# Two-layer graph network on one Trainium2 core: Layer 0 counts its first 208 edge tiles, edge attributes are turned before they are masked, and a node block's tables are made in one burst

## The chip, the cores and the metric

The kernel runs on one core of one Trainium2 chip. The metric is the device time of one execution in microseconds (us), lower is better. Engines are called as in the profile: PE (TensorE matmul), PEld (its weight loads), DVE (VectorE), ACT (ScalarE), POOL (GpSimd), SP (the engine that here only issues DMAs).

## The reference

There are 3,125 nodes with 128 features and 100,000 edges, sorted by destination. The destinations are drawn as 3125·u² with u uniform, so low node numbers have very many edges (node 0 alone has over 1,700) and the destinations advance slowly at first. Cut to what matters:

```
# Layer 0: mean of the source rows, one linear layer, ELU, residual, layer norm
summed = segment_sum(x[src], dst);  deg = segment_sum(1, dst)
x = layernorm(x + elu((summed / max(deg, 1)) @ W + b))
# Layer 1: relational attention, R = 4 edge types, H = 4 heads of C = 128 (HC = 512)
xl = x @ W_l[r] + b_l[r];  xr = x @ W_r[r] + b_r[r]            # tables, one row per node and type
e  = edge_attr @ W_e[type, :16] + rel_emb[type] @ W_e[type, 16:]
z  = leaky_relu(xl[src, type] + xr[dst, type] + e, 0.2)
score = sum_c z[h, c] * att[type, h, c]
alpha = softmax of score over the edges with one (dst, type)
agg[dst, type] += alpha * xl[src, type]
# mean over heads, a softmax gate over types, layer norm, FFN, two layer norms
```

## The kernel before

Edges are cut into 784 tiles of 128, four of them a **quad** (196 quads). The function `windows` has four stages.

**Prologue.** Index arrays are loaded, turned so that an edge lies on a partition (`src_e`, `loc_e`, `typ_e`), and a flag is worked out that says whether the index data satisfy what the fast path assumes. If not, a general path runs after it.

**Layer 0**, a loop over steps `s`, one quad a step. POOL gathers the 128 source rows of each tile by an indirect DMA into a ring `xg` of 24 tiles (`gather`). A one-hot of the destinations (`onehot4`, tile `oh`) multiplies the gathered rows (`sums0`, PSUM tile `sg`), ACT copies the sums (`sgs`), a second one-hot (`spread0`, `ohq`) spreads them to 64 nodes (`out0`, PSUM tile `fo`), and DVE adds that to the running sums of all nodes (`add0`, `acc0`). `sums0` of a quad frees its four ring places, and only then are the next four gathers issued.

Beside that the same loop prepares Layer 1:
- Edge attributes: `load_chunk` loads 112 tiles' attributes at a time (`earow`, seven chunks; the last has 109 full rows), `turn_chunk` transposes them and splits each into a high and a low part, 32 values an edge (`ees`). For each quad `masked` copies the 32 values to the four types' places and zeroes those of the other types (DVE, `em`, 128 x 512), `turned` transposes the four tiles (four PE transposes into `mp`, an ACT copy to `emt`), and `keep` writes 256 KB to DRAM (`eam_d`).
- Node blocks: as soon as the sums of 128 nodes are complete (`behind(b)` says after which quad), `block` runs its parts in following steps: `take`, `mean` (linear layer on PE), an exponential on ACT, `stats`, a square root on ACT, `scaled`, `turn` (transpose to `ht`). Then `lin` makes 16 columns and `table(r)`, one type a step, makes the two tables of a type: two matmuls 128x128x512 into `xp`, a DVE addition of the bias `cl` to the left one, a DVE addition of `cb` to the right one (`xf`), an ACT rounding of it (`xh`), and a step later in `half(r)` DVE's remainder. The tables go to DRAM (`xl_d`, `xr_d`).

The order on each of PE, DVE, ACT, POOL and SP is written out by hand: the class `Ordered` chains all instructions of an engine in the order in which the program issues them (all have line 647 in the profile). Jobs are put at a step by `at_step`.

**Attention**, again one quad a step, in a software pipeline. `load_rows` loads for the next quad the masked attributes `ea` (four buffers), the segment row `sg` (three buffers), `rm` and the windows of the right table `win` (14 buffers), all on SP's queue; `load` gathers the left table's rows on POOL. For each head `z_of` sums on PE two attribute matmuls (`weh`, `wel` by `ea`), the window matmuls by the one-hot `oht` and four transposes, into one of three PSUM tiles `z`; ACT applies `relu`; PE makes the scores (`row`). DVE does the softmax by scans (`local1` .. `joined4`), PE and DVE the weighted sums.

**Tail**: the final norms and the feed-forward layer over 25 node blocks.

Of the kernel before, what the change touches and what calls it, by code (L numbers as in the profile page):

```python
# [20 lines left out]
P = 128  # L21
# [640 lines left out]

def windows_of(u):
    k = 4 if u < UQ else 2 if u < UP else 1
    return [(i, k) for i in range(0, 4, k)]
# [15 lines left out]
def windows(ctx: ExitStack, tc: tile.TileContext, a, out, flag):  # L681
# [7 lines left out]
    eam_d = dram.tile([NQ, P, 512], F32, name="eam_d")  # L689
# [5 lines left out]
    xli_e = S["xli_e"] = cst.tile([P, TT], I32, name="xli_e")  # L695
# [10 lines left out]
    tng = cst.tile([P, TT, R], BF16, name="tng")  # L706
# [35 lines left out]
    with tc.tile_pool(name="l0c", bufs=1) as l0c:  # L742
        acc0 = l0c.tile([P, 2, NPW], F32, name="acc0")
        src_e = l0c.tile([P, TT], I32, name="src_e")

        XG = 24
        xg = l0c.tile([P, XG, F + 1], F32, name="xg")
        nc.vector.memset(xg[:, :, F:], 1.0)
        pool = Ordered(tc, nc.gpsimd)
# [5 lines left out]
        with tc.tile_pool(name="pr", bufs=1) as pr, tc.tile_pool(name="prp", bufs=2, space=PSUM) as prp:  # L755
# [26 lines left out]

            srci = rows("srci", "src", 0, nc.scalar)
# [7 lines left out]
            bad = pr.tile([P, 8], F32, name="bad")  # L791
# [3 lines left out]
            nc.vector.memset(acc0, 0.0)  # L795

            src = floats("src", srci)
            to_e(src_e, src)
            for t in range(XG):
                gather(t)  # L800
# [25 lines left out]
            rF, rL, rB = (rfl[:, i] for i in range(3))  # L826
            wt = prp.tile([TR, TC], F32, name="fp_")
# [9 lines left out]
            nc.vector.tensor_copy(d0_i, rB[0:1])  # L837
            typ = floats("typ", typi)
            to_e(typ_e, typ)
            tm = l0c.tile([P, TT, R], BF16, name="tmr")  # L840
# [5 lines left out]
            nc.vector.scalar_tensor_tensor(seg, loc, float(R), typ, op0=OP.mult, op1=OP.add)  # L846
# [23 lines left out]
            rF4, rL4 = (x[0:1].rearrange("p (u i) -> p u i", i=4) for x in (rF, rL))  # L870
            for j, (w, x, y) in enumerate((
# [4 lines left out]
                count(1 + j, n)  # L876

# [7 lines left out]
            bp = prp.tile([1, 8], F32, name="bp", bufs=1)  # L885
# [18 lines left out]
        with tc.tile_pool(name="m0c", bufs=1) as m0c, tc.tile_pool(name="l0", bufs=2) as l0, \  # L904
# [4 lines left out]
            one = l0e.tile([1, 1], F32, name="one")  # L909
            nc.vector.memset(one, 1.0)  # L910
# [12 lines left out]
            fb = l0e.tile([P, TT], F32, name="fb")  # L923
# [4 lines left out]
            cl = m0c.tile([P, R, XW], F32, name="cl")  # L928
            cb = m0c.tile([P, R, HC], F32, name="cb")
# [11 lines left out]
            def load_table_weights():  # L941
# [4 lines left out]
                sp.dma_start(cl[:, :, :HC], bass.AP(tensor=a["L1_gnn_b_l"].tensor, offset=a["L1_gnn_b_l"].offset,  # L946
                                                    ap=[[0, P], [HC, R], [1, HC]]))
# [30 lines left out]
            def rows_of_sources():  # L978

                ve.tensor_scalar_min(xli_e, typ_e, float(R - 1))  # L980
                ve.scalar_tensor_tensor(xli_e, src_e, R, xli_e, op0=OP.mult, op1=OP.add)
                ve.tensor_scalar(tng, tm, 1.0, BIG, op0=OP.subtract, op1=OP.mult)

            def linear_weights(r, w):
                def f():
# [3 lines left out]
                    tmp = m0.tile([P, HC], F32, name="tmp", bufs=1)  # L989
                    ve.tensor_mul(tmp, w[:, r, :HC], at_)  # L990
                    ve.tensor_reduce(w[:, r, HC:XW], tmp.rearrange("p (h c) -> p h c", h=H), AX.X, OP.add)
                    ve.tensor_scalar(w[:, r, HC:XW], w[:, r, HC:XW], SLOPE, None, op0=OP.mult)
                return f

            def constant(r):
                def f():
# [3 lines left out]
                    cp = bank().rearrange("p a b -> p (a b)")  # L1000
                    pe.matmul(cp, cr[:, r:r + 1].to_broadcast([DR + 1, P]), cw, start=True, stop=True)
                    act.activation(cb[:, r], cp, AF.Copy)
# [3 lines left out]
            for i, f in enumerate([edge_weights, rows_of_sources] +  # L1006
                                  [linear_weights(r, w) for r in range(R) for w in (wl, cl)] +
                                  [constant(r) for r in range(R)]):
                at_step(4 + i, "ve", f)
# [186 lines left out]
            for s in range(last + 1):  # L1196
# [3 lines left out]
                if s < NQ:  # L1200
                    turned(s)
# [484 lines left out]
```

## Time and profile before

| | |
|---|---|
| median of 3 runs | 3265.17 us (3262.53 to 3267.92) |
| the profiled execution | 3014.4 us, span 3012.6 us |
| mean granted TensorE clock in the profiled execution | 0.851 |
| prologue, to the first `sg` matmul | 64.3 us |
| Layer 0, first to last `sg` matmul | 64.3 to 1154.7 us |
| first `z` matmul of attention | 1236.5 us |
| last addition of attention | 2892.1 us |

The profiled execution is 250.8 us shorter than the median of the timed runs. Busy times and durations below are of the profiled execution. In a window's answer a row gives each engine's busy time and, in brackets, its number of instructions; a float32 matmul is shown as two instructions.

### The profile page before, as it was taken

To read this page: it belongs to the slowest core of one execution; us is meant where nothing else is said; L and a number is where in the kernel's file an instruction comes from. 1 tells how busy PE (TensorE), PEld (TensorE's weight loads), DVE (VectorE), ACT (ScalarE), POOL (GpSimd) and SP (SyncE) were. 2 spreads that over 40 slices of the span, in tenths; PEclk is the share of its full clock that TensorE was granted. 3 is DMA by queue.
4 is the path that set the end of the run, shared out by engine and by line. 5 is a ranking of instruction groups with operands and counts; after the bars stand their busy time and mean duration, and the time that the engine had idled before them with its cause. 6 is when DMAs were issued, how large, how long until landed. Compare 5 with 4: busy or idle time off the path is not lost.

```text
span 3012.6 us, 69650 instructions
## 1 busy us (share of the span) xinstructions
PE 2521.1 (84%) x25681; PEld 1858.9 (62%) x25681; DVE 1794.3 (60%) x6092; ACT 867.3 (29%) x1872; POOL 1552.6 (52%) x1578
## 2 busy tenths in 40 slices
PE   2867777767567777699999999999999999999952
PEld 1444444434244343477777777888888888788832
DVE  6523445455455565367666667667666666566667
ACT  1212223233233232233333333333333333233211
POOL 5777777777756650444444444444444444444200
PEclk9555667677767687899999999999999999999956
DMA  5433545465445554777777777888888899999710
GB/s 154 141 111 98 162 140 184 162 202 186 154 172 191 174 185 169 271 225 221 221 227 221 222 224 231 256 257 255 255 258 252 255 260 259 245 253 258 189 34 23
DMA packets 278166, 599.24 MB, mean 199 GB/s; under 512 B 47142, under 2 KB 98647, under 8 KB 273820
## 3 DMA queue, kind: packets, MB, share of 16 engines
q1 hardware_dynamic: 186568, 334.42, 34.2%
q0 software_dynamic: 87808, 258.61, 30.5%
q8 instruction: 206, 3.38, 0.5%
q10 hardware_dynamic: 3440, 1.66, 0.3%
q14 instruction: 144, 1.17, 0.1%
HBM read 460.02 MB, written 134.48 MB: 197 GB/s over the span
## 4 chain that ended last, share of the span: by engine, by line
PE 50%; DMA 6%; DVE 3%; issue 0%; SPq 0%; ACT 0%; DVEq 0%; ACTq 0%
PE z L647 30%; PE row L647 9%; PE ag L647 6%; DMA win<-xr_d 4%; PE fo L647 2%; PE sm_p L647 2%; DMA ea<-eam_d 1%; DMA out_dram<-o 0%; DMA fh_all<-fh_d 0%; DMA rm<-rm_d 0%; PE hm L1640 0%; DVE fst L1599 0%; PE xp L647 0%; DMA xr_d<-xh 0%; SPq L647 0%
## 5 line engine op out<-in xcount | busy, mean ns | idle before, releaser
L647 POOL DMA_INDIRECT xl<-xl_d,xli_e x784 | 754.0, 962 | 958.3 <-DVE r L647 326.1
L647 POOL DMA_INDIRECT xg<-in_x_dram,src_e x784 | 797.4, 1017 | 323.0 <-issue 132.0
L647 ACT ACTIVATE relu<-z 128x512 f32<-128x512 f32 x784 | 468.4, 597 | 1104.5 <-PE z L647 1102.7
L647 PE MATMUL z<-f_ident,xl 128*128 128x128 f32 x3136 | 475.6, 274 | 0.0
L647 PEld LDWEIGHTS z<-f_ident,xl 128*128 128x128 f32 x3136 | 368.5, 141 | 44.5 <-issue 0.6
L647 PE MATMUL z<-ea,weh 128*128 128x512 f32 x784 | 383.9, 490 | 12.6 <-DMA sg<-seg_d 12.6
L647 PE MATMUL z<-oht,win 96*128 96x128 f32 (+2 forms) x1600 | 346.9, 298 | 16.5 <-DMA win<-xr_d 16.2
L647 PEld LDWEIGHTS z<-oht,win 128*128 128x128 f32 (+1 forms) x1600 | 276.8, 190 | 77.0 <-DMA win<-xr_d 10.3
L647 PE MATMUL z<-ea,wel 128*128 128x512 f32 x784 | 311.3, 397 | 0.0
L647 PE MATMUL fo<-ohq,sgs 128*128 128x64 f32 x784 | 168.3, 357 | 164.2 <-ACT sgs L647 68.5
L647 PE MATMUL sg<-xg,oh 128*32 128x129 f32 x1568 | 200.6, 361 | 122.8 <-DMA xg<-in_x_dram,src_e 120.7
L647 PEld LDWEIGHTS fo<-ohq,sgs 128*128 128x128 f32 x784 | 153.7, 274 | 193.0 <-ACT sgs L647 130.7
L647 PE MATMUL row<-relu,attw 128*32 128x128 f32 x6272 | 248.5, 276 | 0.0
L647 PEld LDWEIGHTS sg<-xg,oh 128*32 128x32 f32 x1568 | 64.5, 126 | 281.6 <-DMA xg<-in_x_dram,src_e 184.3
L647 DVE TENSOR_TENSOR oh<-loc_e,iw 128x128 f32<-128x128 bf16 (+1 forms) x294 | 99.1, 337 | 217.1 <-PE sg L647 216.7
L647 PE MATMUL ag<-xl,wo 128*32 128x128 f32 x6272 | 218.8, 280 | 3.4 <-DVE wo L647 3.4
L647 PEld LDWEIGHTS z<-ea,weh 128*128 128x128 f32 x784 | 148.1, 189 | 89.6 <-issue 89.5
L647 PE MATMUL mp<-f_ident,em 128*128 128x128 f32 x784 | 178.8, 369 | 11.0 <-issue 5.1
L647 ACT ACTIVATE xh<-xf 128x512 fp32r<-128x512 f32 x100 | 63.0, 630 | 431.5 <-DVE xf L647 257.1
L647 PEld LDWEIGHTS row<-relu,attw 128*32 128x32 f32 x6272 | 164.0, 110 | 32.7 <-issue 32.7
L647 PEld LDWEIGHTS ag<-xl,wo 128*32 128x32 f32 x6272 | 164.4, 112 | 7.2 <-DVE wo L647 3.7
L647 DVE TENSOR_TENSOR acc<-acc,fo 128x128 f32 (+1 forms) x392 | 99.5, 254 | 115.0 <-issue 44.1
(270 smaller groups left out, 3602.4 us busy)
## 6 DMA issues: line engine op xcount, KB each, us to landing
win<-xr_d SPq DMA_DIRECT2D x224, 256.0 KB
xr_d<-xh SPq DMA_DIRECT2D x100, 512.0 KB
eam_d<-emt SPq DMA_DIRECT2D x196, 256.0 KB
ea<-eam_d SPq DMA_DIRECT2D x196, 256.0 KB
win<-xr_d SPq DMA_DIRECT2D x176, 192.0 KB
xl_d<-xlr SPq DMA_DIRECT2D x25, 1032.0 KB
sg<-seg_d SPq DMA_DIRECT2D x196, 128.0 KB
rm<-rm_d SPq DMA_DIRECT2D x392, 32.1 KB
```

What stands on the lines that cost most here:

```text
L647: ins = f(*args, **kw)
```

## The change

- **Counting.** For the first 52 quads (`UD`, 208 tiles; all destinations below `ND` = 240) no rows are gathered. `count` makes for each tile a one-hot of the source's low 7 bits (`ol`, 128 x 128) and one of the pair source block and destination (`oc`, 128 x 200, from quad 24 on 128 x 300), and one bf16 matmul a tile counts into PSUM `dn`; `count_add` adds a quad's counts to a matrix `A` (128 x 25 x 252) at a column read into a register. When all are counted, `counted_sums` multiplies the 25 blocks of `x` with `A` and adds the result to `acc0`. The flag gets three more conditions. The Layer 0 loop has 144 steps for the other quads; the 52 counts are put on steps 3 to 41, two, one and one to a step; the multiplications follow from step 43 on, and blocks 0 and 1 come after them.
- **Attributes turned unmasked.** One transpose turns a quad's four tiles of 32 values; four quads share one ACT copy and are written as four DMAs of 64 KB (`eat_d`). In attention a load repeats the 32 rows for the four types (`er`, two buffers), ACT makes the distance of the segment row from the row's type (`far`, one buffer), and DVE's `masked` multiplies by a comparison of it (`ea`, now two buffers).
- **Tables in one burst.** All eight table matmuls of a block come in one step (`tables`), each preceded by a matmul that adds the bias from a two-part float32r row (`two`, `cbl`). ACT copies the tables out of PSUM (`xh`, `xlr`), the DVE additions go, the four `half` come in the next step between DVE's other work, and `xl_d` is written in four DMAs.
- **Order.** ACT's copy of the last quad's sums (`out_copy`) comes first in the next step.

```
+UD, ND, SHI = 52, 240, NB2
+def counted(u):
+    return 8 if u < 24 else 12
...
-            for t in range(XG):
+            for t in range(TD, TD + XG):
                 gather(t)
...
-            def masked(u):
...
-            def turned(u):
-                mp, m = bank(), X.pop(("em", u))
-                for q in range(4):
-                    pe.transpose(mp[:, q], m[:, q].rearrange("p r x -> p (r x)"), ident)
-                em = X["emt", u] = l0.tile([P, 4, P], F32R, name="emt", bufs=4)
+            def turned(us):
+                mp = bank()
+                for j, u in enumerate(us):
+                    c, i0 = u // QC, u * 4 % TR
+                    pe.transpose(mp[:, j], ees[c][:, i0:i0 + 4].rearrange("p t s d -> p (t s d)"), ident)
+                em = l0.tile([P, 4, P], F32R, name="emt", bufs=3)
                 act.activation(em, mp, AF.Copy)
...
+            def count(u):
+                w = counted(u)
+                cn = l0p.tile([P, SHI, w], F32, name="dn")
+                for i in range(4):
+                    t = 4 * u + i
+                    ol = l0.tile([P, P], BF16, name="ol", bufs=4)
+                    ve.tensor_scalar(ol, il, lo_f[:, t:t + 1], None, op0=OP.is_equal)
+                    oc = l0.tile([P, SHI * w], BF16, name="oc", bufs=4)
+                    ve.tensor_scalar(oc, ic[:, :SHI * w], c_f[:, t:t + 1], None, op0=OP.is_equal)
+                    pe.matmul(cn.rearrange("p a b -> p (a b)"), ol, oc, start=(i == 0), stop=(i == 3))
+            def count_add(u):
+                n = nc.values_load(dc_i[0:1, u:u + 1], engines=[ENG.DVE], min_val=0, max_val=ND - 1, ...)
+                v = A[:, :, ds(n, counted(u))]
+                ve.tensor_tensor(v, v, X.pop(("cn", u)), op=OP.add)
+            def counted_sums(k):
+                pe.matmul(X["dn"][:, 0], X.pop(("xc", k)), A[:, k, :ND], start=(k == 0), stop=False, ...)
...
+            C0 = 3
+            for u in range(UD):
+                at_step(C0 + u * 3 // 4, "count", u)
...
-                def lin():
-                def table(r):
-                    ve.tensor_add(d["xlr"][:, r, :HC], xp, cl[:, r, :HC])
-                    ve.tensor_add(d["xf", r], xq, cb[:, r])
-                    act.activation(d["xh", r][:, 0], d["xf", r], AF.Copy)
+                def tables():
+                    xa = m0p.tile([P, R, H], F32, name="mw")
+                    pe.matmul(xa, two[:, 0], cbl[:, :, HC:], start=True, stop=False)
+                    pe.matmul(xa, d["ht"], wl[:, :, HC:], start=False, stop=True)
                     for r in range(R):
+                        xp, xq = (m0p.tile([P, HC], F32, name="xp", bufs=3) for _ in range(2))
+                        for o, w, i, c in ((xq, wr[:, r], 1, cbl[:, r, :HC]), (xp, wl[:, r, :HC], 0, cbl[:, r, :HC])):
+                            pe.matmul(o, two[:, i], c, start=True, stop=False)
+                            pe.matmul(o, d["ht"], w, start=False, stop=True)
+                        act.activation(xh[:, 0], xq, AF.Copy)
+                        act.activation(xl[:, :HC], xp, AF.Copy)
+                        act.activation(xl[:, HC:], xa[:, r], AF.Copy)
...
+                block(b, max(behind(b) - UD, C2 + 4 * b if b * P < ND else 0) + 1)
...   (the loop's order in a step)
+                u = UD + s
+                sp jobs; out_copy(u - 1); turned(...); first half; onehot4(u + 1); second half; spread0(u); other halves
+                out0(u - 1); count(v); add0(u - 1); count_add(v); act and ve jobs; sums0(u); burst; keep(...)
...
-            d["ea"] = at.tile([P, 512], F32R, name="ea", bufs=4)
-            sp.dma_start(d["ea"].bitcast(F32), eam_d[u])
+            d["er"] = at.tile([P, 512], F32, name="er", bufs=2)
+            sp.dma_start(d["er"], bass.AP(tensor=ev.tensor, offset=ev.offset, ap=[[0, R], [512, 2 * DE], [1, 512]]))
...
+        def distance(u):
+            d["far"] = at.tile([P, 512], BF16, name="far", bufs=1)
+            act.activation(d["far"], d["sg"], AF.Abs, bias=pm)
+        def masked(u):
+            d["ea"] = at.tile([P, 512], F32R, name="ea", bufs=2)
+            ve.scalar_tensor_tensor(d["ea"], d["far"], 16.0, d["er"], op0=OP.is_lt, op1=OP.mult)
...
             part(load, s, 0, 1, NQ)
+            part(distance, s, 0, 1, NQ)
...
             part(joined3, s, 7, 2, NGR)
+            part(masked, s, 0, 1, NQ)
             part(spread, s, LATE, 1, NQ)
```

## The prediction

> **What bounds the kernel now.** I read the page's slices first, for the stages:
>
> ```profile
> PE   2867777767567777699999999999999999999952
> ...
> POOL 5777777777756650444444444444444444444200
> PEclk9555667677767687899999999999999999999956
> ```
>
> A slice is 75 us. Attention (slice 17 on) is full on PE at full clock; Layer 0 is full nowhere, and PE runs there at half to three quarters of its clock. Then the windows of Layer 0, for its pace:
>
> ```profile
> 602.00:678.00 76.00, 52.98 (x284) 29.99 (x282) 41.26 (x110) 22.82 (x47) 58.02 (x60) 0.79 0.60 201
> 678.00:753.00 75.00, 60.00 (x315) 35.70 (x316) 43.28 (x116) 24.50 (x50) 57.45 (x58) 0.78 0.54 186
> 753.00:828.00 75.00, 38.24 (x193) 20.99 (x190) 32.91 (x83) 16.08 (x33) 53.82 (x54) 0.72 0.46 154
> 828.00:904.00 76.00, 52.64 (x250) 30.86 (x250) 38.58 (x104) 22.89 (x47) 45.17 (x45) 0.70 0.49 171
> ```
>
> The fifth pair is POOL. Up to 753 us it issues 58 gathers in 75 us: 1.29 us each, 5.2 us a quad, the same from 75 us on. POOL is the bound there. Later it issues 45: it waits for ring places. The groups of 850 to 1150 us (count, then busy and mean ns, then idle before them) say for what:
>
> ```profile
> L647 POOL DMA_INDIRECT xg<-in_x_dram,src_e x172 | 176.2, 1024 | 97.3 <-PE sg L647 51.9 <-issue 36.3 <-PE mw L647 4.9
> L647 PE MATMUL xp<-wl,ht 128*128 128x512 f32 x76 | 61.2, 899 | 0.0
> L647 PE MATMUL xp<-wr,ht 128*128 128x512 f32 x76 | 55.9, 827 | 0.0
> L647 PE MATMUL fo<-ohq,sgs 128*128 128x64 f32 x188 | 38.5, 340 | 71.9 <-ACT sgs L647 38.3 <-DVE acc L647 31.4 <-DVE mv L647 2.2
> L647 PE MATMUL mp<-f_ident,em 128*128 128x128 f32 x192 | 37.3, 326 | 0.6 <-DVE em L647 0.6
> L647 DVE TENSOR_TENSOR em<-ee,tmr 128x512 f32<-128x512 f32 x47 | 32.1, 683 | 0.0
> L647 ACT ACTIVATE emt<-mp 128x512 fp32r<-128x512 f32 x48 | 28.4, 591 | 4.0 <-PE mp L647 3.4
> ```
>
> 48 quads in 300 us are 6.25 us each, and 152 `xp` instructions are 76 matmuls, 9.5 blocks, 31.6 us a block. PE itself idles 72 us ahead of `fo`. So this half is bound by the chain sums, ACT copy, spread, addition, lengthened by the tables. A step without table work took 2.6 us (`sg` at 837.98, next at 840.57), so a block costs 31.6 - 5.05 x 2.6 = 18.5 us on the chain. There is also one hole: `fo` after 802 us waited 33.8 us, while a load of 109 rows (872 KB) moved at about 26 GB/s.
>
> For attention, the waits of DVE, 1300 to 2480 us (total, times, longest):
>
> ```profile
> DVE m L647 <- PE row L647: 149.7, 73, 2.4
> ...
> DVE dx L647 <- ACT jx L647: 63.3, 73, 1.6
> ...
> DVE dd L647 <- ACT p L647: 55.8, 73, 0.9
> ```
>
> In each pair of steps DVE waits 2.05, 0.87 and 0.76 us: that is the room for new DVE work.
>
> [...] 0.50 in 75 to 151 us, 1.00 in attention; table matmuls followed each other every 1.9 us after a pause (1205 us) and every 0.86 us in a dense run (1209 to 1215 us). [...] the trace of before has no Abs.
>
> **Part by part, in the profiled execution's own time (3014.4 us).**
>
> *Gathers.* 208 x 1.29 = 268 us leave POOL. POOL alone would then need 576 x 1.29 = 743 us. Whether the 268 are gained depends on what the chain can do, so I sum the chain.
>
> *Start.* Added on DVE ahead of the first sums: clearing `A` (6,300 columns; the 6,528 of `acc0` took 5.5 us), clearing `cbl` (1.5 by the same rate), seven small column operations and more flag counts (about 3.5), less two `em` (1.3). First `sg` at 73 us instead of 64. The ring is full by then; POOL waits.
>
> *Steps 0 to 41, with the counts.* Per tile DVE makes `ol` and `oc`. No row shows a bf16 to bf16 one-hot this size. [...] the nearest rows are `ohq` 128x64 float32 at 0.25 and `oht` 128x512 at 0.48. I take 0.45 us for the two, bounds 0.33 and 0.65. A quad is 1.8, its register load and `count_add` 0.7 (as `acc`, 0.29 and a gap of 0.3), the wait for the last matmul 0.4: 2.9 us, times 4/3 a step = 3.9. The step's own `oh`, `ohq`, `acc` make 1.0. So 4.9 us, 191 for 39 steps, and DVE, not POOL, sets the pace. Jobs that were covered by POOL now count: edge, left and constant weights with their ACT round trips about 31, eight `turn_chunk` 20, three early blocks 16 each = 48 (DVE part, halves, and waiting for PE in the burst). Sum 290: step 42 at 363 us. `em` (0.68 a step) is already out. PE's counts (208 bf16 matmuls[...]) and the 25 loads of `x` lie beside this.
>
> *Steps 42 to 143.* A step without table: `sg` 0.6, ACT copy with its latencies 0.65, `fo` 0.9: 2.2 us; the four transposes and their copy, which now come once in four quads, took most of the 0.4 difference to 2.6. A block: eight matmuls at 0.86 = 6.9, eight float32r bias matmuls at 0.28 (the spacing of `wel` in attention) = 2.2, [...] the 16 columns 0.6, ACT's last copies ahead of the next `sgs` 0.8, mean and turn 1.8: 14 us, bounds 11 (warm) and 18 (as now). What is saved against 18.5 is the half clock and ACT's `sgs` standing behind `xh`; the bias matmuls give part of it back. ACT's twelve copies a block, 5.9 us (0.63, 0.60, 0.25), and DVE's four halves (0.69) run beside the burst, three `xp` banks suffice at these times. So 102 x 2.2 = 224, 20 blocks x 14 = 280, 25 counted matmuls 22, sixteen `turn_chunk` 20. The 109-row load is issued at step 98 and the next block's `x` load stands behind it: 25 of the 34 us (bounds 0 and 35). Sum 571: last `sg` at 934 us, against 1154.7: **221 us less**. POOL's own line would be 363 + 96 x 5.2 = 862, so the chain, not POOL, ends last.
>
> *To attention.* From the last `sg` to the first `z` 82 us now: 21 us for three blocks' tables in half-clock bits go to three bursts; 15 us less (bounds 30 less, 10 more). SP issues more, smaller DMAs (75 more `xl_d`, 25 `x`, 32 small rows, each 0.3 to 0.8 us) in a queue that is mostly idle; `keep` moves a quarter of the bytes.
>
> *Attention.* DVE's `masked` 128x512: 0.69 us (`e`, the same operation at 128 columns, 0.29, and 384 columns at 0.96 a ns), 196 times = 135 us, in even steps just before the wait for `jx` (0.87), in odd steps before that for `p` (0.76): covered by these waits. If that cover were gone, `oht` and the next `ea` would be late next. `ea` is ready some 1.8 us before the next step's first `z`. `distance` on ACT 0.6 us falls in the wait of over 1.5 us ahead of `relu(u, 0)`; it queues before that relu, so a late `sg` now stops ACT as well as DVE. `er` has two buffers where `ea` had four, so SP's loads of a quad, `sg`, `rm` and `win` behind it, go out about half a step later: `sg` keeps some 1.4 steps (11 us) ahead. The bytes are the same. In the last 400 us, where DMA is over 90% busy, that costs something: 10 us taken (bounds -5 and 60).
>
> Sum: 3014.4 - 221 - 15 + 10 = 2788, **225 us less**. The timed median is 250.8 us above the profiled execution, which no row explains; I carry the difference over unscaled: 3265 - 225 = **3040**.
>
> **Rivals.**
> - *The chain is cheaper and POOL still bounds* (block 11 us, counts at their low bound): last `sg` at about 862, 72 us earlier: 2968. For it: DVE is busy under half of Layer 0 and loses `em`, PE loses three transposes in four. Against: the written order puts PE's sums of a step behind DVE's counts of it in steps 3 to 41. Chance 0.17.
> - *The burst runs cold and the early steps cost more*: 20 blocks x 4 = 80 us, counts at 0.65 x 208 instead of 0.45 = 42: 3160. Chance 0.24.
> - *Attention gets a new wait, slower than before*: place: `ea(u)` by `distance` and `masked` ahead of `z_of(u, 0)`. If both (0.6 + 0.69) were on the path in each of 196 steps: 253 us more instead of 10, 3283. It decides from (225 + 10)/196 = 1.2 us a step. Against: the waits above, and a dense PE at 1.00. Chance 0.08.
> - *It does not do what it says*: the new flag conditions would send the data to the general path too. From the inputs the quads span at most 4 (limit 8) and 9 (limit 12) destinations and tile 207 ends at 218: excluded.
>
> **How the numbers follow.** My case has 0.51, alone 2990 to 3090. Faster by over 0.2% (6.5 us, about what a measurement here can tell from none) are this case and the first two rivals, less a little for unknown stalls: 0.90; within 0.2% 0.02; slower 0.08. The range takes in both faster rivals: 2940 to 3165.
>
> **What would show it.** Right: POOL's gathers 576; first `sg` near 73; step 42 near 363 with DVE 80% busy before it; last `sg` near 934; `xp` under 700 ns mean; attention's stretch within 2% of 1656 us with PE full. Wrong: PE below 95% between 1300 and 2480 us of before's stages, `z` waiting for DVE `ea`, or ACT `far` waiting for DMA `sg`; or Layer 0's last `sg` after 1050.

## The result and the profile after

The kernel after takes **3244.13 us** (median of 5 runs, 3235.3 to 3246.55) beside 3265.17 us for the kernel before (median of 5): a ratio of 0.9929, interval 0.9911 to 0.9946. It is 21 us (0.7%) faster; 225 were predicted, and the time lies above the range. The profiled execution has a span of 3243.3 us, 3245.12 us with what lies around it.

One thing is needed to read any number here. The kernel before itself took 3014 to 3024 us in its first profile and in the first four experiments, and 3265 to 3292 us everywhere else, the first comparison included; one chip gave both (e1 and e12). What makes the difference is not known; it is called the occasion below, and times are compared on one occasion only. The kernel before was profiled on both kinds, and this table has its stages on both. They are read from the first and last start of `sg` and of the attribute matmuls into `z`; attention is the time from the first to the last of these `z`, and the last column is the span:

| kernel, occasion | last `sg` | first `z` | last `z` | attention | span |
|---|---|---|---|---|---|
| before, 3024 us occasion | 1155.3 | 1237.2 | 2857.6 | 1620 | 3014.0 |
| before, 3286 us occasion | 1319.7 | 1397.0 | 3121.7 | 1725 | 3277.0 |
| after, 3265 us occasion | 1113.0 | 1187.3 | 3086.3 | **1899** | 3243.3 |

On like occasions, though on two chips, the change takes some 207 us out of Layer 0 (221 predicted) and puts some 174 us into attention (10 predicted).

The slices of the page after, for the same three rows as before (a slice is now 81 us):

```profile
PE   1456666655566658999999999898999989988853
...
POOL 5455545455355232444444444444444433333200
PEclk9976676766667778999999999999999998898966
```

Before, PE stood at 9 from slice 17 to the end of attention; now it falls to 8 again and again, and from slice 33 on the granted clock dips too. POOL, which issued at 7 tenths through two thirds of Layer 0, stands at 5 or less: 576 gathers instead of 784. The windows (pairs in the order PE, PEld, DVE, ACT, POOL; then PEclk, DMA share, GB/s) say how much:

```profile
602.00:678.00 76.00, 40.49 (x196) 25.35 (x194) 18.42 (x64) 15.93 (x36) 43.29 (x47) 0.57 0.37 111
...
828.00:904.00 76.00, 46.69 (x203) 27.42 (x202) 18.92 (x65) 21.99 (x50) 37.91 (x40) 0.66 0.44 144
1300.00:1600.00 300.00, 282.81 (x3572) 219.44 (x3573) 204.72 (x719) 111.06 (x238) 132.75 (x135) 0.98 0.73 203
...
2000.00:2400.00 400.00, 364.66 (x4611) 296.49 (x4601) 255.46 (x899) 136.56 (x294) 168.28 (x168) 0.95 0.75 216
```

In these windows of Layer 0 no engine is busy for even two thirds of the time; POOL issues 47 and 40 gathers where it issued 60 and 45, so POOL no longer bounds either half. In attention PE loses 17 of 300 us and 35 of 400; in the profile before it lost none, and on the 3286 us occasion 15 in the last of these windows. At the same time the DMA share is no higher (0.73 and 0.75; in the same windows before 0.76 and 0.84, on the other occasion 0.80 in the last), so the mean share does not show that loads come late. The waits of the attention stage (1300 to 3080 us: total, times, longest) name what is late:

```profile
ACT far L647 <- DMA sg<-seg_d: 534.8, 115, 11.5
ACT relu L647 <- PE z L647: 356.7, 306, 4.3
DVE oht L647 <- DMA sg<-seg_d: 321.9, 73, 10.3
...
DVE m L647 <- PE row L647: 69.1, 38, 3.0
```

ACT's `far` waits for the segment row `sg` 115 times in 535 us of this stretch, and DVE's `oht` for the same load. DVE's wait for `row`, 174 us in the profile before over the same stretch, is down to 69: DVE is now held by something else. The chain that ended last (by engine, then by line) says that these waits lie on the path. In the profile before it was

```profile
PE 50%; DMA 6%; DVE 3%; issue 0%; SPq 0%; ACT 0%; DVEq 0%; ACTq 0%
PE z L647 30%; PE row L647 9%; PE ag L647 6%; DMA win<-xr_d 4%; PE fo L647 2%; PE sm_p L647 2%; DMA ea<-eam_d 1%; DMA out_dram<-o 0%; DMA fh_all<-fh_d 0%; DMA rm<-rm_d 0%; PE hm L1640 0%; DVE fst L1599 0%; PE xp L647 0%; DMA xr_d<-xh 0%; SPq L647 0%
```

and in the profile after

```profile
PE 40%; DMA 25%; DVE 11%; another core or an unknown queue 8%; issue 7%; ACT 4%; SPq 2%; DVEq 0%; ACTq 0%
DMA sg<-seg_d 17%; PE z L647 15%; PE xp L647 7%; PE row L647 5%; PE fo L647 4%; DMA er<-eat_d 4%; PE ag L647 2%; SPq L647 2%; PE sg L647 2%; DMA win<-xr_d 1%; PE mp L647 1%; PE dn L647 1%; DMA rm<-rm_d 1%; PE mw L647 1%
```

The load of `sg`, not in the list before, is 17% of the span, and `z` is down from 30% to 15%. For Layer 0 the groups of 850 to 1150 us shown before have this counterpart in the kernel after, 850 to 1100 us:

```profile
L647 POOL DMA_INDIRECT xg<-in_x_dram,src_e x133 | 125.5, 944 | 115.4 <-PE sg L647 75.0 <-issue 29.4 <-remote 8.2
L647 PE MATMUL xp<-cbl,two 128*128 128x512 f32 x60 | 51.8, 863 | 5.8 <-ACT xlr L647 3.6 <-DVE xh L647 2.2
L647 PE MATMUL xp<-wr,ht 128*128 128x512 f32 x60 | 38.0, 721 | 0.0
...
L647 PE MATMUL fo<-ohq,sgs 128*128 128x64 f32 x140 | 31.5, 366 | 64.6 <-ACT sgs L647 32.6 <-issue 26.1 <-ACT mv L647 3.5
```

`xp` is cheaper than before (0.72 us for the right table instead of 0.83), and PE still idles ahead of `fo`. The 0.86 us of a bias matmul are not its price, since successive instructions of PE overlap in the profile: before, in the dense run of 1209 to 1215 us, table matmuls shown as 1.02 us long start every 0.86 us. In the burst at 639 us a bias matmul starts every 1.08 us (639.24, 640.33, 641.41, 642.50), with the two `xp` instructions of its table in between.

### The profile page after: what moved, and what is told of

It reads as the page before. It is cut to its first block, busy times and chain, and to the rows that moved or that the text cites. A ratio compares the mean times of both kernels' runs of the same rounds, so it can differ in the third digit from the quotient of the medians.

```text
span 3243.3 us, 67735 instructions
## 1 busy us (share of the span) xinstructions
PE 2474.8 (76%) x24804; PEld 1828.0 (56%) x24804; DVE 1730.9 (53%) x6219; ACT 945.0 (29%) x2071; POOL 1340.8 (41%) x1371
## 4 chain that ended last, share of the span: by engine, by line
PE 40%; DMA 25%; DVE 11%; another core or an unknown queue 8%; issue 7%; ACT 4%; SPq 2%; DVEq 0%; ACTq 0%
DMA sg<-seg_d 17%; PE z L647 15%; PE xp L647 7%; PE row L647 5%; PE fo L647 4%; DMA er<-eat_d 4%; PE ag L647 2%; SPq L647 2%; PE sg L647 2%; DMA win<-xr_d 1%; PE mp L647 1%; PE dn L647 1%; DMA rm<-rm_d 1%; PE mw L647 1%
## 5 line engine op out<-in xcount | busy, mean ns | idle before, releaser
L647 POOL DMA_INDIRECT xl<-xl_d,src_e x784 | 778.2, 993 | 1193.8 <-PE ag L647 290.7
L647 POOL DMA_INDIRECT xg<-in_x_dram,src_e x576 | 561.0, 974 | 526.6 <-PE sg L647 308.5
L647 PE MATMUL fo<-ohq,sgs 128*128 128x64 f32 x576 | 137.6, 384 | 267.7 <-ACT sgs L647 164.8
L647 ACT ACTIVATE far<-sg,pm 128x512 bf16<-128x512 bf16 x196 | 141.3, 721 | 646.9 <-DMA sg<-seg_d 546.4
L647 DVE TENSOR_SCALAR oht<-sg,p 128x512 fp32r<-128x512 bf16 x196 | 95.9, 489 | 386.6 <-DMA sg<-seg_d 330.8
L647 PEld LDWEIGHTS fo<-ohq,sgs 128*128 128x128 f32 x576 | 116.6, 284 | 319.4 <-ACT sgs L647 204.0
L647 DVE TENSOR_TENSOR acc<-acc,fo 128x64 f32 (+1 forms) x340 | 84.0, 247 | 393.6 <-PE fo L647 122.6
L647 PE MATMUL xp<-cbl,two 128*128 128x512 f32 x200 | 176.8, 884 | 41.2 <-ACT xlr L647 25.4
L647 DVE TENSOR_TENSOR xh<-xp,xh 128x512 fp32r<-128x512 f32 x100 | 69.1, 691 | 223.5 <-ACT xh L647 177.9
L647 PEld LDWEIGHTS z<-ea,wel 128*128 128x128 f32 x784 | 156.7, 200 | 4.6 <-issue 4.5
```

What stands on the lines that cost most here:

```text
L647: ins = f(*args, **kw)
```

## The experiments

Two theories came first: the **lead theory**, that `er`'s two buffers hold back the loads queued behind `er` on SP (the prediction had named this place, at 10 us), and the rival that the loads land late on some occasions whatever the kernel does. The first four kernels ran on the 3024 us occasion.

**e1, the kernel before again.** No edit.

> The kernel before, unchanged, profiled again. Its first profiled execution took 3014.4 us and its timed runs 3265, so either theory about the attention stage has to be told first which of the two is usual. Lead theory (in the kernel after, er's two buffers hold back the loads queued behind it on SP; the kernel before has no such wait): the profile shows attention (first z to last z) at about 1656 us with PE 100% busy whatever the total is, and 250 us more lie elsewhere or nowhere. State theory (the DMAs of attention land later in most executions, in both kernels): a profile of about 3265 us has attention near 1900 us, with DVE oht waiting for DMA sg as in the kernel after.

Measured: 3024.5 us, ratio to itself 1.0006 (0.9993 to 1.0019); attention 1620 us, PE full. On this occasion the kernel before has hardly any late loads (DVE's `oht` waits for `sg` 17 times, 54 us in sum); the other occasion stayed open until e12.

**e2, `er` loaded last.**

```
 def load_rows(u):
-    d["er"] = at.tile([P, 512], F32, name="er", bufs=2)
-    sp.dma_start(d["er"], ... [[0, R], [512, 2 * DE], [1, 512]])
     d["sg"] = ...; rm; win ...
+    d["er"] = at.tile([P, 512], F32, name="er", bufs=2)
+    sp.dma_start(d["er"], ... [[0, R], [512, 2 * DE], [1, 512]])
```

> The kernel after, with one edit: load_rows issues sg, rm and the windows of a quad first and er last. er has two buffers, so its load waits for masked of two quads before, and in the kernel after sg and win of the same quad stand behind that wait on SP. Lead theory: sg of the next quad then goes out a step earlier (lead 2.4 steps instead of 1.4), ACT far and DVE oht hardly wait for DMA sg (under 60 us in sum instead of 535 and 322), attention comes down from 1903 to 1660 to 1720 us and the total to 3000 to 3070 us. State theory (landing times are longer in themselves): total 3220 to 3250 us.

Measured: 2914.0 us, 0.9647 (0.9618 to 0.9676), last `sg` 854.7, attention 1816 us. Half a hit: the wait for `sg` is gone, as the lead theory says, but its place is taken by `er` itself. DVE and ACT waits of e2, 1300 to 2700 us:

```profile
DVE ea L647 <- DMA er<-eat_d: 172.5, 61, 8.7
...
ACT far L647 <- DMA sg<-seg_d: 13.7, 2, 7.5
```

`er` was issued 15 us ahead of its use in the median, about a step and a half, and still came late 61 times. So the order of the loads is not the cause, and the lead hardly; the load itself looks slow.

**e3, the kernel before with the new attributes alone.**

```
-    masked(u): em = ee * (type == r);  turned(u): four transposes;  keep(u): 256 KB to eam_d
+    turned(us): one transpose a quad;  keep(us): 64 KB a quad to eat_d
-    d["ea"] (4 buffers) <- eam_d[u]
+    d["er"] (2 buffers) <- eat_d[u], four times;  far = |sg - type|;  ea = (far < 16) * er
```

> The kernel before, with only the attribute part of the change: attributes turned unmasked with one transpose a quad, spread to the four types by the load of er, and masked in attention by far and masked. No counting, no bursts, no biases on TensorE. Lead theory: attention 1890 to 1910 us as in the kernel after, Layer 0 shorter by about 0.3 us a quad (60 us at most), total against the kernel before on the same chip +180 to +240 us if that is at its 3014, and near 0 if the 250 us already lie in its attention. State theory: total within 60 us below the kernel before.

Measured: 3289.4 us, 1.0876 (1.0834 to 1.0918); last `sg` 1159.5, attention 1884 us. This part of the change alone, with the numbering of segment rows that `far` needs, costs 263 us in attention. In the kernel before it gains nothing in Layer 0 (1155.3 in e1), where up to 60 us were expected; so the total is 266 us longer and not 180 to 240. The rival that blamed the occasion falls: the loads are late in this kernel where they are not in e1.

**e4, the kernel after with the old attributes.** The opposite edit of e3, with `em` and `emt` at two buffers and a ring of 20 tiles for room.

```
+    masked(v), turned(v), keep(v): em, four transposes, 256 KB   (ready tiles in Layer 0)
+    d["ea"] = at.tile([P, 512], F32R, name="ea", bufs=4);  sp.dma_start(d["ea"], eam_d[u])
-    er, far, masked in attention
-    XG = 24
+    XG = 20
```

> The kernel after with the attribute part taken back: attributes masked in Layer 0 (em, four transposes a quad), ea loaded ready with four buffers, no far and no masked in attention. To make room in Layer 0 em and emt have two buffers and the ring of gathered rows 20 places instead of 24. Lead theory: attention back to about 1660 us, Layer 0 longer than in the kernel after by 0.7 to 1.3 us a quad (some 100 to 180 us), total 3080 to 3190 us. State theory: attention stays near 1900, total 3330 to 3420 us.

Measured: 2839.5 us, 0.9400 (0.9372 to 0.9428); last `sg` 991.1, attention 1618 us. Attention is that of the kernel before; Layer 0 is 164 us shorter than in e1 and 136 longer than in e2: what unmasking is worth once the gathers no longer bound Layer 0, the smaller ring and buffers of this kernel included.

The next four ran on the 3287 us occasion.

**e5, the kernel after, unchanged.**

> The kernel after, unchanged, beside the kernel before on the same chip. In the kernel with er last, Layer 0 is word for word that of the kernel after, and its last sg came at 854.7 us instead of 1113.0 in the profile after; so some 250 us of that profile's Layer 0 would belong to the occasion (the chip or how its memory lay), as the 250 us between the profile of before (3014) and its timed runs (3265) would. Occasion theory: last sg 850 to 870 here, attention still about 1890 us by er's buffers, total 2970 to 3010 us. Program theory (the order of SP's loads, which differs in attention alone, somehow delays Layer 0, by other addresses of tiles or instructions): last sg near 1110 again, total 3235 to 3250.

Measured: 3246.6 us, 0.9884 (0.9856 to 0.9911); last `sg` 1119.2, attention 1893 us. Because the occasion was the slower one for all four kernels, it says nothing for or against the program theory; e2 and e12 do.

**e6, `er` and `ea` one tile of four buffers.**

```
-    d["er"] = at.tile([P, 512], F32, name="er", bufs=2)
+    d["ea"] = at.tile([P, 512], F32R, name="ea", bufs=4)      # same load, same order
-    d["ea"] = at.tile(..., bufs=2);  ea = (far < 16) * er
+    ea = (far < 16) * ea
```

> The kernel after with er and ea made one tile of four buffers, masked in place: the same far, the same masked, the same loads in the same order, and as much memory as er 2 and ea 2. Only the number of buffers that a load may run ahead differs: four, as the kernel before has. Buffer theory: attention 1620 to 1660 us, PE 100% busy, ACT far waits for DMA sg under 40 us; total 2690 to 2750 us. Work theory (far on ACT and masked on DVE stand in the way in themselves): attention 1750 us or more, total over 2820.

Measured: 3232.7 us, 0.9827 (0.9802 to 0.9852); attention 1870 us, 23 less than e5. A miss, for 1620 to 1660 were expected: **the lead theory falls**. With four buffers, as many as the kernel before has, the waits are still there (1300 to 3080 us):

```profile
ACT far L647 <- DMA sg<-seg_d: 446.8, 92, 11.4
...
DVE oht L647 <- DMA sg<-seg_d: 271.4, 62, 10.0
```

**e7, the in-place kernel without counting.**

```
-UD, ND, SHI = 52, 240, NB2
+UD, ND, SHI = 0, 240, NB2
-    count_columns(); count, count_add; x_load, counted_sums; dc_i; three flag conditions
```

> The in-place kernel without the counting: all 784 tiles are gathered and summed, no A, no counted matmuls, no extra loads of x. Bursts, biases on TensorE and attributes unmasked stay. What the counting is worth: by the working of the prediction POOL then needs 784 x 1.29 = 1011 us after 19 us and bounds Layer 0: last sg at 1030 to 1060 us against about 855, total 170 to 210 us over the in-place kernel. If instead the chain's own price were the bound, last sg would come at 64 + 196 x 2.2 + 25 x 14 = 850 us, about the same as with counting.

Measured: 3490.0 us, 1.0607 (1.0577 to 1.0637); last `sg` 1401.0 against 1139.9 in e6. The positions were expected for the other occasion, so only the difference reads: 261 us in Layer 0, where 170 to 210 were expected of the total (it is 257). The 208 gathers at 1.29 us that leave POOL are 268.

**e8, the in-place kernel with tables spread.**

```
-                at_step(s + 7, "burst", tables)            # all four types
-                for r in range(R): at_step(s + 8, "half", half(r))
+                for r in range(R):
+                    at_step(s + 7 + r, "burst", tables(r)); at_step(s + 8 + r, "half", half(r))
```

> The in-place kernel with the tables of a block issued one type a step over four steps, as the kernel before does, instead of in one burst; the biases stay on TensorE (one extra copy of 16 columns a block). Burst theory (a dense burst runs at full clock and keeps the chain's other steps free): without it xp's means rise to 1.1 to 1.4 us and last sg comes 60 to 120 us later than about 855. Rival (the 768 ns per matmul and the ACT copies cost the same wherever they stand): within 25 us.

Measured: 3132.9 us, 0.9531 (0.9511 to 0.9550), 100 us less than e6, and last `sg` at 1058.0 against 1139.9. Both expectations miss: with spread tables Layer 0 is 82 us *shorter*. In the burst of 639 to 647 us of the profile after the granted clock is 1.00, in the 11 us before it 0.55; but spread, `xp` did not get dearer: 0.82, 0.77 and 0.69 us for bias, right and left table (375 to 1140 us), 0.92, 0.76 and 0.73 in e6.

By now `er`'s order, its lead and its buffers were ruled out, and e2 had it slow in itself. What was left is the form of the load. SP's issues of `rm` and of `ea` in the kernel before (from e12; minimum, median, maximum in ns):

```profile
L647 SPq DMA_DIRECT2D rm<-rm_d x392: 143/584/878, 1394.8 to 3083.8; - x196
```

```profile
L647 SPq DMA_DIRECT2D ea<-eam_d x196: 319/331/788, 1394.0 to 3090.1; - x196
```

and of `rm` and `er` in the kernel after:

```profile
L647 SPq DMA_DIRECT2D rm<-rm_d x392: 582/662/3997, 1179.2 to 3055.4; - x196
```

```profile
L647 SPq DMA_DIRECT2D er<-eat_d x196: 2/612/895, 1178.0 to 3063.8; - x196
```

The load of the same 256 KB takes SP nearly twice as long to issue, and an `rm` issue that never took 0.9 us now takes up to 4.0: SP stands still in the middle of issuing. `ea`'s pattern leads with 128 rows, `er`'s, `[[0, R], [512, 2 * DE], [1, 512]]`, with R = 4. The **engine theory** of the next expectations is that `er` is slow by this form alone. Engines are in its name only: no profile here names the engine of a DMA, so what was tried is the effects of the form. e9 to e12 ran on one chip, on the 3286 us occasion.

**e9, the load of `er` in four.**

```
-            sp.dma_start(d["er"], bass.AP(tensor=ev.tensor, offset=ev.offset,
-                                          ap=[[0, R], [512, 2 * DE], [1, 512]]))
+            for r in range(R):
+                sp.dma_start(d["er"][r * 32:(r + 1) * 32], ev)
```

> The kernel after, with one edit: the load of er is four DMAs of 32 rows (one for each type) instead of one whose access pattern has the four copies outermost. Bytes, buffers (er 2, ea 2), far, masked and the order of SP's loads stay. Engine theory: [...] (an rm issue of up to 4.4 us, sg up to 7.3 us, against 0.8 and 1.5 in the kernel before). [...] rm issues under 1 us again, ACT far and DVE oht wait for DMA sg under 60 us, attention 1630 to 1700 us instead of 1890, total 190 to 260 us below the kernel after. Buffer theory (two buffers give too short a lead however fast the load is): attention 1800 us or more.

Measured: 3091.8 us, 0.9406 (0.9368 to 0.9443); attention **1730 us**, 5 more than the kernel before on this chip (e12). That is 155 us below e5, where 190 to 260 were expected, and 30 above the expected attention, which had been set by the kernel before's attention on the other occasion; the buffer theory's 1800 is far off. Its chain:

```profile
PE 69%; issue 8%; DVE 6%; another core or an unknown queue 6%; ACT 3%; DMA 3%; SPq 2%; DVEq 0%; POOL 0%; ACTq 0%
PE z L647 32%; PE row L647 9%; PE xp L647 9%; PE ag L647 6%; PE fo L647 5%; PE sg L647 2%; SPq L647 2%; PE dn L647 2%; PE sm_p L647 1%; PE mp L647 1%; PE mw L647 1%; DMA xl<-xl_d,src_e 1%; ACT L647 1%; ACT sgs L647 1%
```

its waits in 1300 to 3080 us:

```profile
ACT relu L647 <- PE z L647: 558.2, 367, 3.1
...
DVE m L647 <- PE row L647: 256.5, 94, 3.6
...
ACT far L647 <- DMA sg<-seg_d: 1.5, 1, 1.5
```

and its `rm` issues:

```profile
L647 SPq DMA_DIRECT2D rm<-rm_d x392: 143/592/871, 1201.0 to 2911.1; - x196
```

`sg` is gone from the chain, `far` waits for it once instead of 115 times, DVE waits for `row` again, and no `rm` issue takes 0.9 us. One load in another form gives back 160 us or more (e16: 1890, profile after: 1899). As the two buffers and all of `far` and `masked` are still there, neither of these is the main cause.

**e10, the store in rows of 32 too.**

```
-                for j, u in enumerate(us):
-                    sp.dma_start(eat_d[u].rearrange("x (t e) -> t x e", t=4), em[:, j])
+                for t in range(4):
+                    sp.dma_start(eat_d[us[0]:us[0] + 4, :, t * P:(t + 1) * P].rearrange("j x e -> x j e"),
+                                 em[t * 32:(t + 1) * 32])
```

> As the kernel with er split, and the store of attributes too: keep issues for each of the four tiles of a quad one DMA of 32 rows over four quads, instead of for each quad one DMA whose outer size is 4. The same number of DMAs and bytes. Engine theory: attention as with er split; in Layer 0 the eight stores that took SP 18.6 us to issue at 645.83 us (profile after) go out in under 6 us, and last sg comes up to 60 us earlier than in the kernel with er split. If the stores never stood in the way: within 10 us of it.

Measured: 3068.8 us, 0.9347 (0.9310 to 0.9383); last `sg` 1102.5, 30 us earlier than in e9. The 18.6 us of the expectation were a misreading: one row of the profile joins two groups of four stores, in which SP issued for about 3 and 2 us, with 13 us between them in which it issued nothing. What did change is the single issue, 0.44 us in the median instead of 0.52, and the longest, behind the 109-row load, 3.8 instead of 12.7 us. The times of e9 and e10 overlap in their intervals, but the last `sg` of the three runs with this store and the burst (e10, e11, e15) lies at 1097 to 1103 us, and with the old store (after, e5, e6, e9, e16) at 1113 to 1140. So the store's form is worth some 10 to 40 us of Layer 0; by which wait, no run shows.

**e11, e10 with `er` and `ea` in one tile of four buffers.** The edit of e6 on e10.

> As the kernel with er and keep split, and er and ea one tile of four buffers, masked in place. What the two buffers cost once the load is fast: by the waits, a lead of 1.4 steps (11 us) instead of 3. If the engine theory holds alone, within 15 us of the kernel with two buffers; if buffers count too, 20 to 60 us below it.

Measured: 3087.0 us, 0.9386 (0.9343 to 0.9429), 18 us above e10 with overlapping intervals: outside both expectations, and no gain. Its attention is 1756 us, 29 more than in e10, for which no cause was found. Buffers are not what attention lacked.

**e12, the kernel before on that chip.**

> The kernel before, unchanged, profiled on the same chip as the other three. Two occasions have been seen: one with this kernel at 3024 us, one at 3265 to 3287. If this is the slower one, the profile shows for the first time where its 250 us lie: occasion theory: in Layer 0, as waits that end by no semaphore of the profile (issue, remote), attention within 40 us of 1621. If attention is longer by 100 us or more here too, slow landing of loads belongs to the occasion and not to er.

Measured: 3292.2 us, 1.0021 (1.0003 to 1.0039). The profile shows both: last `sg` 164 us later than in e1, attention 104 us longer. The waits in 60 to 1150 us that the profile puts down to another core or an unknown queue, the longest three sums:

```profile
ACT sgs L647 <- remote: 194.5, 44, 9.3
...
DVE oh L647 <- remote: 121.9, 34, 7.4
...
DVE acc L647 <- remote: 90.5, 19, 8.2
```

e1 has not one such wait in that stretch. So the slower occasion costs the kernel before 164 us in Layer 0 and 104 in attention. By the letter of the expectation, 104 us would lay the slow loads to the occasion and not to `er`. The waits say otherwise (1300 to 3080 us of e12):

```profile
DVE oht L647 <- DMA sg<-seg_d: 4.4, 1, 4.4
```

`sg` is late once here, and e9 on the same chip and occasion differs from the kernel after in the form of one load. With `er` in one load the occasion hits other places: Layer 0 is 258 us longer in the profile after than in e2, whose Layer 0 is the same, and attention only 6 to 15 (1890 and 1899 against 1884 in e3). What lies behind "remote" was not tried.

The last four ran on another chip, the kernel before at 3290 us. e9 had changed two things at once, the outer size and the reading of one 64 KB block by one DMA four times.

**e13, the kernel before, with `ea` loaded by a pattern of outer size four.**

```
-    eam_d = dram.tile([NQ, P, 512], F32, name="eam_d")
+    eam_d = dram.tile([NQ, R, 33, 512], F32, name="eam_d")
-            sp.dma_start(d["ea"].bitcast(F32), eam_d[u])
+            sp.dma_start(d["ea"].bitcast(F32), bass.AP(tensor=ev.tensor, offset=ev.offset,
+                                                       ap=[[33 * 512, R], [512, 32], [1, 512]]))
```

(and the store as four DMAs of 32 rows.)

> The kernel before, with one thing of the kernel after: the load of ea has an access pattern with the four types outermost (their blocks in memory lie 33 rows apart[...]), as the load of er has. Its 256 KB are all different, nothing is read four times; four buffers; no far, no masked, seg and sg as before. The store to that layout is four DMAs of 32 rows, which adds issues on SP in Layer 0. Engine theory: [...] attention grows by 130 to 270 us against the kernel before, rm issues of over 3 us appear on SP, total +130 to +280 us. Re-reading theory (er is slow because the same 64 KB are read four times) or work theory (far and masked): attention within 30 us of the kernel before.

Measured: 3419.8 us, 1.0394 (1.0365 to 1.0424); last `sg` 1314.4, attention **1866 us**, 141 more than in e12; the timed runs, 130 more than the kernel before on the same chip, so at the low end of what was expected. Its SP issues and one of its waits (1450 to 3240 us):

```profile
L647 SPq DMA_DIRECT2D rm<-rm_d x392: 13/667/3941, 1393.3 to 3236.0; - x196
```

```profile
L647 SPq DMA_DIRECT2D ea<-eam_d x196: 3/615/1486, 1392.1 to 3243.6; - x196
```

```profile
DVE oht L647 <- DMA sg<-seg_d: 213.5, 47, 8.8
```

The form of the load alone, with 256 KB of different data, four buffers and no masking, makes the issues as slow as in the kernel after, lets `sg` come late, and costs 141 us. Re-reading and masking are excluded as the main cause.

No trace names the engine of a packet, but the traces keep the start, duration, queue and size of every DMA packet, and so show how many are in flight at once. The 109-row load of the prediction's hole has one packet in flight for 35 of its 39 us, and never more than two (profile before). The first load of attention stands ahead of all other packets of 2 KB on SP's queue; the first 128 of these packets give:

| run | form of the load | its packets took | most in flight | time with at most four |
|---|---|---|---|---|
| profile before | one DMA, outer size 128 | 1.3 us | 19 | 6% |
| e12, before | one DMA, outer size 128 | 1.5 us | 20 | 15% |
| e9 | four DMAs of 32 rows | 2.5 us | 16 | 40% |
| after | one DMA, outer size 4 | 4.9 us | 7 | 86% |
| e13 | one DMA, outer size 4, all rows different | 3.7 us | 6 | 89% |

Exactly four are in flight for 79% of the time in the profile after, for 2% in e12 and 1% in the profile before. So the load with outer size 4 has at most four packets in flight most of the time (86 and 89%), and its packets took 4.9 and 3.7 us where those of the load with outer size 128 took 1.3 and 1.5. How many engines carry it is not shown.

**e14, e10 with tables spread**, the edit of e8 on e10.

> The kernel with er and keep split, and in addition the tables of a block one type a step instead of in one burst (biases still on TensorE). With the burst in the in-place kernel, last sg came at 1139.9 us, spread at 1058.0, total 100 us less. If that is the burst's own price (PE, ACT and DVE of the chain stand behind 14 us of it), 60 to 110 us below the kernel with er and keep split[...].

Measured: **2985.9 us, 0.9081 (0.9031 to 0.9132)**, 75 us below its partner e15; last `sg` 1035.9 against 1098.9, attention 1722 us in both. That is within the 60 to 110 us expected of the burst's own price; the store can't explain it, since e15 has the same one. It beats both kernels, and has the lowest ratio of all runs.

**e15, e10 again.**

> The kernel with er and keep split, again, as the partner of the spread kernel on one chip, and, should this be the quicker occasion (kernel before at 3024 us), to see whether attention comes back there as well. Engine theory: on the quicker occasion attention 1621 to 1640 us (it was 1885 with er in one load) and last sg near 855, total 2680 to 2730 us; on the slower one 3069 us as before.

Measured: 3061.0 us, 0.9314 (0.9282 to 0.9347), attention 1722 us; 3069 were expected on the slower occasion, and the quicker one did not turn up.

**e16, the kernel after again.**

> The kernel after, unchanged, again, as the partner of these on one chip. On the slower occasion 3247 us. On the quicker one, not seen yet: last sg near 855 as in the kernel with er last, attention 1885 as in the kernel before with the new attributes, total 2970 to 3010 us.

Measured: 3247.3 us, 0.9873 (0.9837 to 0.9910), as expected; attention 1890 us, on one chip with e15 and 168 us more. The quicker occasion for the kernel after stays unmeasured. An estimate from e1, the Layer 0 of e2 and the attention of e3: 3024 - 301 + 263 = some 2990 us, which would also be about 1% faster.

## Why the prediction was wrong, step by step

**Attention: the step that failed.** The prediction put "The bytes are the same" and took 10 us, bounds -5 and 60. They are the same bytes, in another form. The prediction had a slow load before its eyes, the 109 rows of Layer 0 at about 26 GB/s, and did not ask whether the new load's form would make that one slow as well: `er`'s outer size is 4, `ea`'s 128. Measured: 165 us (e16 against e12, on two chips with the kernel before at 3286 and 3290), 263 us on the quicker occasion (e3 against e1). e9 gives all but 5 us back by the form of the load alone, e13 makes 141 us of it in the kernel before, and the packets show at most four in flight for 86% of the time (after) where it was 15% (e12). How that stretches SP's other issues to 4.0 us is not shown. With that one load in four, the change is worth 194 us (e9 against the kernel before on its chip), with the store 217, where the prediction has 225.

**The two-buffer lead.** The prediction saw that `sg` would keep only 11 us ahead and named the sign that would prove it wrong, "ACT `far` waiting for DMA `sg`". The sign came; the reason was another. With four buffers the waits stay (e6), with two buffers and the load in four DMAs they go (e9: once, 1.5 us) or are few (e10: 18 times, 66 us, with no longer attention).

**`far` and `masked`.** Right: 0.72 us on ACT (0.6 predicted) and 0.68 us on DVE (0.69; the 0.96 columns a ns in it are what rows of before show, 0.69 us for 128x512 of `xh` and 0.29 for 128x128 of `acc`), covered by the waits named: with both in place e9, e10 and e15 have attention within 6 us of the kernel before. The new Abs brought no more table loads on ACT: 50 in the profile after, 52 before, 1.28 us each. The rival "attention gets a new wait", the one that ended slower, had the right stage, and the wrong mechanism: not two operations on the path, but a load and what waits behind it on SP. That its 253 us lie near the 263 of e3 is chance.

**Layer 0: right in direction, its size near by luck.** The 221 us were worked out on the quicker occasion, and there 301 are measured (e2 against e1): step 42 comes at 311 us instead of 363, and from there to the last `sg` it takes 544 instead of 571. The 207 us on the slower occasion (after against e12) come nearer, but are made with waits that the sum doesn't have. Its terms, on the quicker occasion:
- Start: first `sg` at 73 predicted, 72.0 and 72.3 measured.
- Counts: step 42 at 363 us predicted; the last addition to `A` came at 308 (e2), 370 in the profile after. `ol` and `oc` are 0.246 and 0.286 us in the median, 0.53 together and not 0.45, which was the author's estimate and stands in no row of the profile before; `A`'s addition is 0.36 to 0.47. So the tile was dearer than taken, and what was charged beside it (31 + 20 + 48 us of jobs, and waits) was too much; which part of it, no run tells. DVE was not 80% busy either, but 56% in 60 to 370 us (172.9 of 310, after) and 62% in e2 (190.7).
- Base step: 2.2 us predicted, 2.24 measured (median in e2 of the steps in which PE does nothing but `sg` and `fo`).
- Block: 14 us predicted; the step with a burst takes 14.0 in e2 with its own 2.24 inside, 15.0 in e16. A table matmul with its bias is 1.08 us in the dense burst, where 0.86 + 0.28 = 1.14 was taken. Of the 14 us the terms of the sum make 12.3; the rest was the author's estimate and is not shown. What the profile before shows is one table matmul every 1.9 us at a granted clock of 0.54 (1205 to 1209 us) and every 0.86 us at 1.00 (1209 to 1215 us); the prediction's 0.50 in 75 to 151 us and 1.00 in attention are the granted clock too. What the sum did not ask is whether a burst is the better form: with spread tables Layer 0 is 63 to 82 us shorter (e14, e8). Which of the waits makes that, no run tells apart; on the quicker occasion it was not tried.
- The 109-row load: 25 us predicted; the step over it, which has a burst too, takes 45.7 us in e2, 31 more than the burst steps beside it. Not foreseen: one addition over the columns of `A` (`as`, 128x6000) takes 10.9 us, once.
- POOL in the second half: right that the chain, not POOL, ends last (POOL issues 40 in 76 us, waiting for `sg`).

**To attention**: 15 us less predicted, 3 less measured (74.3 against 77.3 us), within its bounds.

**The 250.8 us between profile and timed runs** were carried over unscaled, without a reason. e12 finds them in Layer 0 and attention of the kernel before (164 + 104). The kernel after seems to lose about as much, but nearly all of it in Layer 0 (258 and 15, against e2 and e3). That the sums come out alike, no run explains; here the prediction had luck.

**The numbers.** The prediction's own sum is 226 us, not 225, which is of no weight. Sum of the measured parts: -207 - 3 + 174 = -36, and 3277.0 - 36 is 2 us from the span after. The range 2940 to 3165 would have held e9 and e10 on their occasion (3092 and 3069). What was too narrow was the bound of the new load, 60 us, which no view of the profile before supports: its `ea` has another form.

## What to carry to other kernels

When a change keeps a load's bytes and changes its access pattern, read the outermost size of the new pattern first. With 4 in place of 128 it was another load here: the packets of its first load took 4.9 us (after) instead of 1.5 (e12), SP's issue 0.61 instead of 0.33 us; other sizes were not tried. It shows where one doesn't look, in the waits for the other loads of that queue (`sg`) and in the longest issue of a neighbour (`rm`, from 0.9 to 4.0 us), while the mean DMA share goes down (2000 to 2400 us: 0.75 after, 0.80 in e12). And profile the kernel before again on the occasion on which the change is timed, before a difference of stages is read.

## What the runs showed of the hardware that was not expected

- A 256 KB load into 128 partitions with an outer size of 4 instead of 128: SP's issue 0.61 instead of 0.33 us, issues behind it up to 4.0 us, attention 141 us (8%) longer (e13). At most four packets are in flight for 86% of the time (after; 15% in e12), and those of the first such load took 4.9 us instead of 1.5. Four DMAs of 32 rows cost SP 0.41 us each and none of these delays (e9).
- The same program on the same chip took 3024 us on one occasion and 3292 on another (e1, e12). Part of the difference is waits put down to another core or an unknown queue, 194.5 us on ACT's `sgs` alone, of which e1 has none; only this one core runs.
